# One scan instruction instead of two for the transposed states of a selective-scan kernel, their old states added in PSUM

## The chip, the cores and the metric

The kernel runs on one core of a Trainium2 chip. The metric is the device time of one execution in microseconds (us). The engines of the core are called PE (TensorE matmul), PEld (TensorE weight load), DVE (VectorE), ACT (ScalarE), POOL (GpSimd) and SP (SyncE, which issues most of the DMAs). Each runs its own instructions in order and waits for the others on semaphores.

## The reference, cut to what matters

The reference has two layers on an image of 256 x 256 tokens and 128 channels. Layer 0 is attention along the rows. Layer 1 is a two-dimensional selective scan: the tokens, widened to 256 channels, are walked in four orders (rows, columns, and both reversed), 65536 tokens in each. For each order, channel d and state n of 16:

```
delta = softplus(dts + dt_bias)
h[d, n] = exp(delta[d] * A[d, n]) * h[d, n] + delta[d] * x[d] * B[n]     # one token after the other
y[d]    = sum over n of h[d, n] * C[n] + D[d] * x[d]
```

The four outputs are added, normalised, gated and projected back to 128 channels. All of it is float32. The change lies in the recurrence of layer 1.

## The kernel before, in words

Layer 0 and the front of layer 1 (projection, convolution) come first; the scan stage starts some 5.5 ms into the execution and lasts to the end. It walks the four orders one after the other (`ORDER = (2, 1, 3, 0)`). An order has 128 chunks of T = 512 tokens; `steps[q]` is the order k and the first token a of chunk q. A chunk is done in NG = 8 groups (g) of 32 channels. The 128 partitions of a group are 4 quarters of the states times 32 channels, and each partition carries NI = 4 states i, so that 4 x 4 = 16 states are covered. One (q, g) is a step of the main loop (L1133); there are 4 x 128 x 8 = 4096.

The four states of a step lie in one tile `hs` (pool name `bx`) of 128 x 4 x 512. They are made in two ways:

- **States 0 and 1** (NB = 2). PE spreads delta*x over the partitions (`spread_du`, L878, into the PSUM tile `ur`), DVE multiplies it by the replicated B (`times_B`, L888). POOL adds the old state, multiplied by the decay of the first token, to column 0 (L1123). ACT writes the decays exp(delta*A) to the PSUM tile `dA`, 2 x 512 columns, of which column 0 of both states stays zero (L1107). DVE then scans both states in one instruction of 1024 columns (L1189): a zero decay in column 512 cuts the second state off from the first.
- **States 2 and 3**, the transposed ones. ACT forms their products with the tokens on the partitions (`products`, L851, into `bt`), and PE turns them back with four transposes for each state (`turn_back`, L863) into the PSUM tiles `bl0` and `bl1`, one bank and one buffer each. ACT writes their decays to `dAl` in SBUF (`long_decay`, L1107). DVE scans each state by its own instruction of 512 columns (L1172), with the old state `hst` as the initial value.

After its scans, POOL saves the last column of the four states, times `a0x`, in `hst` (L1193) and multiplies `hs` by the replicated C (L1196). `a0x` holds the first token's decay for states 0 and 1 and ones for states 2 and 3 (L797, L822). PE sums the products over the states into `yp` (`sums`, L902), two pieces of a chunk of four parts each.

The order of instructions is written out by hand (`manual_schedule`): a step has four places, n = 0 to 3, and `place = 4 * g + n` counts the 32 of a chunk. At n = 0 and n = 1 the half-scans are issued, each followed by the refill of its bank for the next step; at n = 2 `times_B` of the next step and `spread_du` of the one after; at n = 3 the scan of states 0 and 1. The work around the scan comes at fixed places, ahead of the scan of the place: `prepare` of the chunk after next (transposes `tps` at places 8 and 9, `pb` at 12, `pv` at 17 and 18, softplus at 19, which has its own table load, `tpb` and `tpd` from 27 on), the sums at 4 to 7 and 20 to 23, and `store` (`tpy` at 13 and 15) or, in the last order, `finish`, which also normalises, gates and projects. `SHARE` says how many instructions of `products` ACT issues at each place.

PSUM has 8 banks: `bl0`, `bl1`, `ur` and `yp` have one each, `dA` two, and the tag `mm` two buffers for all else. The weights `xw_in` and `dtw_s` of all four orders are loaded once, at the start of the stage.

Of the kernel before, what the change touches and what calls it, by code (L numbers as in the profile page):

```python
# [8 lines left out]
F32 = mybir.dt.float32  # L9
# [7 lines left out]
P = 128  # L17
# [6 lines left out]
DI = 256  # L24
NS = 16
R = 8
# [40 lines left out]
def attention_and_scan_kernel(  # L67
# [590 lines left out]
    NI = 4  # L658
    NB = 2
    sw = ctx.enter_context(tc.tile_pool(name="sw", bufs=1))  # L660
    xw_in = sw.tile([P, K, 2, R + 2 * NS], F32, name="xw_in")
    nc.scalar.dma_start(xw_in, x_projT)
    dtw_s = sw.tile([R, K, DI], F32, name="dtw_s")
    nc.scalar.dma_start(dtw_s, dt_wT)
    dtb_s = sw.tile([P, K, 2], F32, name="dtb_s")
    nc.scalar.dma_start(dtb_s, dt_b)
    A_s = sw.tile([P, K, 2, 4, NI], F32, name="A_s")
# [49 lines left out]
        v = ap.rearrange("(i p w) d -> p w i d", p=P, w=S)  # L717
        return [v[:, w, :, :] for w in range(w0, w0 + T // S)]

    loaded, prepared, summed, replicas, products_of = {}, {}, {}, {}, {}  # L720

    def load(q):
        k, a = steps[q]
# [7 lines left out]
    def prepare(q):  # L731

        k, a = steps[q]
        xt = loaded.pop(q)
        xs = io.tile([P, 2, T], F32, name="xs", bufs=3)
        tps = []
        for h in range(2):
            yield 8 + h
            tp = sps.tile([P, T], F32, name="tps", tag="mm")
            for j in range(4):  # L740
                nc.tensor.transpose(
                    tp[:, j * P : (j + 1) * P], xt[:, j, h * P : (h + 1) * P], ident
                )
            tps.append(tp)
        for h, tp in enumerate(tps):
            yield 10 + h
            nc.scalar.copy(xs[:, h, ::-1] if k >= 2 else xs[:, h, :], tp)  # L747
        yield 12
        pb = sps.tile([R + 2 * NS, T], F32, name="pb", tag="mm")
        for h in range(2):  # L750
            nc.tensor.matmul(  # L751
                pb, xw_in[:, k, h, :], xs[:, h, :], start=(h == 0), stop=(h == 1)
            )
        yield 14
        bc = io.tile([R + 2 * NS, T], F32, name="bc", bufs=1)
        nc.scalar.copy(bc, pb)
        bc_d = sd.tile([2 * NS, T], F32, name="bc_d")
        nc.sync.dma_start(bc_d, bc[R:, :])
        pvs = []
        for h in range(2):  # L760
            yield 17 + h
            pv = sps.tile([P, T], F32, name="pv", tag="mm")
            nc.tensor.matmul(  # L763
                pv, dtw_s[:, k, h * P : (h + 1) * P], bc[:R, :], start=True, stop=True
            )
# [12 lines left out]
        de0 = io.tile([P, NG, 1], F32, name="de0", bufs=1)  # L778
        if a:
            for j in range(4):  # L780
                nc.sync.dma_start(
                    de0[32 * j : 32 * j + 32],
                    de_d.rearrange("(g c) t -> c g t", c=32)[:, :, 0:1],
                )
        yield 27
        tp = sps.tile([P, 4, R + 2 * NS], F32, name="tpb", tag="mm")
        for b in range(4):
            nc.tensor.transpose(
                tp[:, b, :], bc[:, b * P : (b + 1) * P], ident[: R + 2 * NS, : R + 2 * NS]
            )  # L790
        B_t = io.tile([P, 4, R + 2 * NS], F32, name="B_t")
        tpbs = tp
        first = a0x[:, q % 2, :, :NB]
        tps = []
        for w in range(2):
            if w == 0 and a:
                nc.gpsimd.tensor_tensor(  # L797
                    first,
                    A_s[:, k, :, :, :NB].rearrange("p h q i -> p (h q) i"),
                    de0.to_broadcast([P, NG, NB]),  # L800
                    ALU.mult,
                )
# [12 lines left out]
        duT = io.tile([P, 4, DI], F32, name="duT")  # L815
        for w, tp in enumerate(tps):
            yield 30 + 2 * w
            nc.scalar.copy(duT[:, 2 * w : 2 * w + 2, :], tp)
        prepared[q] = xs, de_d, duT, bc_d, B_t
        yield 33  # L820
        if a:
            nc.scalar.activation(first, first, AF.Exp)  # L822
# [32 lines left out]
                    )  # L855
                    yield

    def turn_back(q, g, i):

        bl = sps.tile([P, T], F32, name=f"bl{i}", bufs=1)  # L860
        bt = products_of[q][i]
        for b in range(4):
            nc.tensor.transpose(  # L863
                bl[:, b * P : (b + 1) * P], bt[:, b, g].rearrange("t j c -> t (j c)"), ident
            )
        return bl

    def spread_delta(q, g):
# [228 lines left out]
    load(2)  # L1097
    begin_sums(0, 0)
    replicating, multiplying, summing = [], [], []
    bls = {(0, 0, i): turn_back(0, 0, i) for i in range(NI - NB)}  # L1100


    dA = sps.tile([P, NB, T], F32, name="dA", bufs=1)
    nc.vector.memset(dA[:, :, 0:1], 0.0)

    def decay(to, q, g, i, t0):
        nc.scalar.activation(  # L1107
            to,
            drs[q, g][:, t0:],
            AF.Exp,  # L1110
            scale=A_s[:, steps[q][0], g // 4, g % 4, i : i + 1],
        )

    def long_decay(q, g, i):
        dAl = wk.tile([P, T], F32, name="dAl")
        decay(dAl, q, g, i, 0)
        dAls[q, g, i] = dAl

    def begin(q, g):
        hs = wk.tile([P, NI, T], F32, name="bx", bufs=7)  # L1120
# [3 lines left out]
        bxs[q, g] = hs  # L1124

    SHARE = (0, 2, 2, 2, 2, 1, 2, 2, 2, 1, 1, 2, 1, 2, 1, 1, 0, 0, 0, 0, 0, 0, 2, 2, 1, 1, 1, 1, 0, 0, 0, 0)
    bxs, dAls = {}, {}
    for i in range(NB, NI):
        long_decay(0, 0, i)
    begin(0, 0)  # L1130
# [2 lines left out]
    for s, (q, g) in enumerate(all_steps):  # L1133
# [5 lines left out]
        for n in range(4):  # L1139
            place = 4 * g + n  # L1140
            if n < NB:
                decay(dA[:, n, 1:], q, g, n, 1)
            if nxt and n in (1, 2):
                long_decay(*nxt, NB + n - 1)
            if place == 0 and q + 2 < NQ:
                add_part(q, prepare(q + 2))
            if place == 1 and q + 1 < NQ:
                multiplying.append(products(q + 1))
            if place == 26 and q + 3 < NQ:
                load(q + 3)  # L1150
            if place == 10 and q + 1 < NQ:
                replicating.append(replicate(q + 1))
            if place == 28:
                evacuate(q, 0)
# [12 lines left out]
            piece(replicating)  # L1167
            for _ in range(SHARE[place]):
                piece(multiplying)
            if n < NI - NB:  # L1170
                i = NB + n
                nc.vector.tensor_tensor_scan(  # L1172
                    hs[:, i, :],
                    dAls.pop((q, g, i)),
                    bls.pop((q, g, n)),
                    0.0 if a == 0 else hst[:, g, i : i + 1],
                    ALU.mult,
                    ALU.add,
                )
                if nxt:  # L1180
                    bls[(*nxt, n)] = turn_back(*nxt, n)
            elif n == 2:
                if nxt:
                    begin(*nxt)
                if s + 2 < len(all_steps):
                    urs[all_steps[s + 2]] = spread_du(*all_steps[s + 2])
            else:
                run = hs[:, :NB, :].rearrange("p i t -> p (i t)")
                nc.vector.tensor_tensor_scan(  # L1189
                    run, dA.rearrange("p i t -> p (i t)"), run, 0.0, ALU.mult, ALU.add  # L1190
                )
# [72 lines left out]
```

## Time and profile before

| | |
|---|---|
| median of 3 runs | 29113.9 us (29111.15 to 29117.76) |
| the profiled execution | 29117.18 us, span 29115.4 us |
| mean granted PE clock | 0.934 |
| busy over the span | PE 87%, PEld 41%, DVE 92%, ACT 83%, POOL 80% |
| busy from 8000 to 20000 us (12000 us) | DVE 99.99%, ACT 92%, POOL 92%, PE 86% |
| DMA | 45.8% of 16 engines on SP's queue, 121 GB/s |

The parts of the scan stage, as the windows of the trace give them (busy us of each engine in the window; the fourth order starts near 23040 us):

```profile
core 0: us, PE busy (x) PEld busy (x) DVE busy (x) ACT busy (x) POOL busy (x), PEclk, DMA share, GB/s
...
11700.00:17500.00 5800.00, 5006.79 (x24601) 2168.01 (x24601) 5798.88 (x4103) 5326.92 (x10122) 5328.31 (x3319) 0.92 0.51 130
17500.00:23100.00 5600.00, 4847.66 (x23794) 2101.33 (x23792) 5599.04 (x3975) 5148.65 (x9784) 5146.00 (x3207) 0.92 0.51 130
23100.00:29115.00 6015.00, 5204.54 (x27327) 2561.11 (x27326) 5897.23 (x5016) 5650.60 (x10730) 5706.02 (x3879) 0.95 0.53 133
```

How to read it: after each engine's busy time stands the number of its instructions; `PEclk` is the clock that PE was granted, as a share of full speed. In the lines of the groups, `out<-in` are the program's tiles, then the shapes and the count, then the busy time and the mean of one in ns, then the idle time of the engine just before them and what ended it. In the lines in order of time the first number is the start in us from the span's start and the second the time to the end of the last of the merged instructions.

### The profile page before, as it was taken

The page shows a single profiled execution, that of the slowest core. Times are in us where ns is not written, and L with a number is a line of the kernel's source. Part 1 is how long each engine was busy: PE and PEld are TensorE (multiplying, and loading weights), DVE is VectorE, ACT ScalarE, POOL GpSimd, SP SyncE. Part 2 cuts the span into 40 slices and gives each one's busy share as a digit, 9 for nine tenths or more (in the row PEclk, how much of TensorE's full clock was granted, in tenths as well). Part 3 has the DMA queues.
Part 4 walks back from the last instruction along what each step waited for, and adds up shares of the span by engine and source line. Part 5 has one row for each costly group of instructions (what it writes and reads, how often), then busy time and mean ns, then how long its engine had stood idle before and what let it go on. Part 6 is the DMA issues. An engine that isn't in the chain of part 4 may idle for free. (4 is left out here: it accounts for less than half of the span.)

```text
span 29115.4 us, 414393 instructions
## 1 busy us (share of the span) xinstructions
PE 25211.6 (87%) x140314; PEld 11908.5 (41%) x140314; DVE 26672.0 (92%) x24930; ACT 24286.8 (83%) x47871; POOL 23266.7 (80%) x14327
## 2 busy tenths in 40 slices
PE   6999989888888888888888888888888888888888
PEld 2555545433333333333333333333333344444444
DVE  8666653599999999999999999999999999999999
ACT  5555542499999999999999999999999999999998
POOL 4222222499999999999999999999999999999999
PEclk8999999999999999999999999999999999999999
DMA  4001015555555555555555555555555555555554
GB/s 155 30 28 30 28 58 174 156 130 130 130 130 130 130 130 130 130 130 130 130 130 130 130 130 130 130 130 130 130 130 130 131 134 134 134 134 134 133 135 125
DMA packets 2737782, 3522.74 MB, mean 121 GB/s; under 512 B 707224, under 2 KB 1824280, under 8 KB 2659744
## 3 DMA queue, kind: packets, MB, share of 16 engines
q1 hardware_dynamic: 2730480, 3478.11, 45.8%
q8 instruction: 1102, 18.06, 0.3%
q10 hardware_dynamic: 5168, 18.12, 0.2%
q14 instruction: 1032, 8.45, 0.1%
HBM read 2689.15 MB, written 806.35 MB: 120 GB/s over the span
## 5 line engine op out<-in xcount | busy, mean ns | idle before, releaser
L1196 POOL TENSOR_TENSOR bx<-bx,C_r 128x2048 f32<-128x2048 f32 x4096 | 18644.2, 4552 | 336.3 <-DVE bx L1189 17.3
L1172 DVE TENSOR_TENSOR_SCAN bx<-dAl,hst,bl 128x512 f32<-128x512 f32 x8128 | 9875.5, 1258 | 0.0
L1189 DVE TENSOR_TENSOR_SCAN bx<-dA,bx 128x1024 f32<-128x1024 f32 x4096 | 9360.9, 2285 | 32.1 <-ACT dA L1107 31.6
L863 PE MATMUL bl<-ident,bt 128*128 128x128 f32 x32768 | 5605.3, 298 | 2280.1 <-DVE bx L1172 2247.7
L851 ACT ACTIVATE bt<-duT,B_t 128x256 f32<-128x256 f32 x16384 | 7394.4, 498 | 0.0
L1107 ACT ACTIVATE dA<-dr,A_s 128x511 f32<-128x511 f32 x8192 | 5598.4, 683 | 1505.8 <-DVE bx L1189 1433.8
L863 PEld LDWEIGHTS bl<-ident,bt 128*128 128x128 f32 x32768 | 3779.5, 149 | 6597.0 <-DVE bx L1172 6120.5
L1107 ACT ACTIVATE dAl<-dr,A_s 128x512 f32<-128x512 f32 x8192 | 5785.3, 712 | 170.3 <-DMA dr<-de_d 145.7
L878 PE MATMUL ur<-xs,spread 128*128 128x512 f32 x8192 | 5113.4, 710 | 410.6 <-DVE bx L888 401.0
L888 DVE TENSOR_TENSOR bx<-B_r,ur 128x1024 f32<-128x1024 f32 x4096 | 4915.1, 1200 | 66.1 <-DMA C_r<-bc_d 39.1
L902 PE MATMUL yp<-bx,gather 128*32 128x512 f32 x32768 | 4847.2, 649 | 68.3 <-POOL bx L1196 68.3
L370 POOL TENSOR_TENSOR at<-at,sm 128x2048 f32<-128x2048 f32 x256 | 922.3, 3603 | 2716.3 <-DVE sm L369 2607.1
L878 PEld LDWEIGHTS ur<-xs,spread 128*128 128x128 f32 x8192 | 1362.7, 209 | 2042.3 <-issue 957.6
L1193 POOL TENSOR_TENSOR hst<-bx,a0x 128x4 f32<-128x4 f32 x4064 | 820.3, 202 | 1272.6 <-DVE bx L1189 1269.3
L902 PEld LDWEIGHTS yp<-bx,gather 128*32 128x32 f32 x32768 | 694.1, 112 | 2445.1 <-issue 1800.0
L362 ACT ACTIVATE at<-at,mx 128x256 f32<-128x256 f32 x2048 | 1016.2, 498 | 474.1 <-DVE mx L358 469.4
L776 POOL TENSOR_TENSOR xs<-delta,xs 128x1024 f32<-128x1024 f32 x512 | 1217.0, 2377 | 45.6 <-ACT delta L770 45.6
L763 PE MATMUL pv<-bc,dtw_s 8*128 8x512 f32 x2048 | 1151.9, 642 | 45.5 <-ACT ys L976 43.4
L389 ACT COPY aT<-atp 128x512 f32<-128x512 f32 x512 | 299.7, 585 | 920.1 <-PE atp L382 581.4
L391 DVE COPY aT<-atp 128x512 f32<-128x512 f32 x512 | 353.7, 691 | 772.9 <-PE atp L382 762.4
L751 PE MATMUL pb<-xs,xw_in 128*40 128x512 f32 x2048 | 981.9, 602 | 19.3 <-ACT xs L747 19.1
L926 PEld LDWEIGHTS tpy<-ident,yo 128*128 128x128 f32 x6144 | 806.6, 192 | 367.3 <-issue 367.3
(168 smaller groups left out, 27475.4 us busy)
## 6 DMA issues: line engine op xcount, KB each, us to landing
dr<-de_d SPq DMA_DIRECT2D x4096, 256.0 KB
C_r<-bc_d SPq DMA_DIRECT2D x2048, 256.0 KB
de_d<-delta SPq DMA_DIRECT2D x512, 512.0 KB
B_r<-bc_d SPq DMA_DIRECT2D x2048, 128.0 KB
xtok<-xc_d SPq DMA_DIRECT2D x256, 512.0 KB
yl<-y_d SPq DMA_DIRECT2D x256, 512.0 KB
xtok<-xc_d SPq DMA_DIRECT2D x512, 256.0 KB
yl<-y_d SPq DMA_DIRECT2D x512, 256.0 KB
```

What stands on the lines that cost most here:

```text
L362: nc.scalar.activation(at[:, h, t, :], at[:, h, t, :], AF.Exp, bias=mx[:, h, t : t + 1], accum_out=sm[:, h, t : t + 1],)
L763: nc.tensor.matmul(pv, dtw_s[:, k, h * P : (h + 1) * P], bc[:R, :], start=True, stop=True)
L776: nc.gpsimd.tensor_tensor(xs, delta, xs, ALU.mult)
L851: nc.scalar.mul(bt[:, b, :, j, :], duT[:, b, :].rearrange("t (g c) -> t g c", c=32), B_t[:, b, n : n + 1],)
L863: nc.tensor.transpose(bl[:, b * P : (b + 1) * P], bt[:, b, g].rearrange("t j c -> t (j c)"), ident)
L878: nc.tensor.matmul(ur, spread[:, g % 4].rearrange("p j c -> p (j c)"), prepared[q][0][:, g // 4, :], start=True, stop=True,)
L888: nc.vector.tensor_tensor(bx[:, :NB, :], replicas[q][0], ur.unsqueeze(1).to_broadcast([P, NB, T]), ALU.mult,)
L902: nc.tensor.matmul(yp[32 * g : 32 * g + 32, :], gather, hc[:, i, :], start=(i == 0), stop=True, skip_group_check=True,)
L1107: nc.scalar.activation(to, drs[q, g][:, t0:], AF.Exp, scale=A_s[:, steps[q][0], g // 4, g % 4, i : i + 1],)
L1172: nc.vector.tensor_tensor_scan(hs[:, i, :], dAls.pop((q, g, i)), bls.pop((q, g, n)), 0.0 if a == 0 else hst[:, g, i : i + 1], ALU.mult, AL ...
L1189: nc.vector.tensor_tensor_scan(run, dA.rearrange("p i t -> p (i t)"), run, 0.0, ALU.mult, ALU.add)
L1196: nc.gpsimd.tensor_tensor(hs, hs, replicas[q][1], ALU.mult)
```

## The change

States 2 and 3 get one scan of 1024 columns as well (at n = 0). For this, column 0 of both decays must be zero and the old state must already be in the scan's input. `bl` becomes one tile of two banks with one buffer, refilled in one go at n = 1. After the four transposes of a state, `turn_back` writes column 0 again with an ordinary matmul of the same products (weights `bt`, moving operand the first column of the identity) and adds the old state with a second matmul (weights the identity, moving operand one column of `hst`). At the first chunk of an order both are left out. `a0x` now holds the decay of the first token for all four states, so that `hst` comes out multiplied for states 2 and 3 too. The decays go to two fixed tiles `dAl0` and `dAl1` (2 x 512 columns each, by the parity of g) from column 1 on. To make room in SBUF, `x_projT` and `dt_wT` are no longer held for all orders, but loaded for each order on SP's queue, at the start of `prepare` of its first chunk.

```diff
-    xw_in = sw.tile([P, K, 2, R + 2 * NS], F32, name="xw_in")
-    nc.scalar.dma_start(xw_in, x_projT)
-    dtw_s = sw.tile([R, K, DI], F32, name="dtw_s")
-    nc.scalar.dma_start(dtw_s, dt_wT)
...
         xt = loaded.pop(q)
+        if a == 0:
+            dtw[k] = io.tile([R, DI], F32, name="dtw", bufs=2)
+            nc.sync.dma_start(dtw[k], dt_wT[:, k, :])
+            xw_in[k] = io.tile([P, 2, R + 2 * NS], F32, name="xw_in", bufs=2)
+            nc.sync.dma_start(xw_in[k], x_projT[:, k])
...
-        first = a0x[:, q % 2, :, :NB]
+        first = a0x[:, q % 2]
...
-                    A_s[:, k, :, :, :NB].rearrange("p h q i -> p (h q) i"),
-                    de0.to_broadcast([P, NG, NB]),
+                    A_s[:, k].rearrange("p h q i -> p (h q) i"),
+                    de0.to_broadcast([P, NG, NI]),
...
-    def turn_back(q, g, i):
-
-        bl = sps.tile([P, T], F32, name=f"bl{i}", bufs=1)
-        bt = products_of[q][i]
-        for b in range(4):
-            nc.tensor.transpose(
-                bl[:, b * P : (b + 1) * P], bt[:, b, g].rearrange("t j c -> t (j c)"), ident
-            )
+    def turn_back(q, g):
+
+        bl = sps.tile([P, NI - NB, T], F32, name="bl", bufs=1)
+        for i, bt in enumerate(products_of[q]):
+            for b in range(4):
+                nc.tensor.transpose(
+                    bl[:, i, b * P : (b + 1) * P],
+                    bt[:, b, g].rearrange("t j c -> t (j c)"),
+                    ident,
+                )
+            if steps[q][1]:
+                nc.tensor.matmul(
+                    bl[:, i, 0:1],
+                    bt[:, 0, g].rearrange("t j c -> t (j c)"),
+                    ident[:, 0:1],
+                    start=True,
+                    stop=True,
+                    skip_group_check=True,
+                )
+                nc.tensor.matmul(
+                    bl[:, i, 0:1],
+                    ident,
+                    hst[:, g, NB + i : NB + i + 1],
+                    start=False,
+                    stop=True,
+                    skip_group_check=True,
+                )
         return bl
...
+    dAls = [sw.tile([P, NI - NB, T], F32, name=f"dAl{e}") for e in range(2)]
+    for dAl in dAls:
+        nc.vector.memset(dAl[:, :, 0:1], 0.0)
...
     def long_decay(q, g, i):
-        dAl = wk.tile([P, T], F32, name="dAl")
-        decay(dAl, q, g, i, 0)
-        dAls[q, g, i] = dAl
+        decay(dAls[g % 2][:, i - NB, 1:], q, g, i)
...
-            if n < NI - NB:
-                i = NB + n
+            if n == 0:
+                run = hs[:, NB:, :].rearrange("p i t -> p (i t)")
                 nc.vector.tensor_tensor_scan(
-                    hs[:, i, :],
-                    dAls.pop((q, g, i)),
-                    bls.pop((q, g, n)),
-                    0.0 if a == 0 else hst[:, g, i : i + 1],
+                    run,
+                    dAls[g % 2].rearrange("p i t -> p (i t)"),
+                    bls.pop((q, g)).rearrange("p i t -> p (i t)"),
+                    0.0,
                     ALU.mult,
                     ALU.add,
                 )
+            elif n == 1:
                 if nxt:
-                    bls[(*nxt, n)] = turn_back(*nxt, n)
+                    bls[nxt] = turn_back(*nxt)
```

The order of all other instructions stays: PE's refill of both halves now stands at n = 1, behind PE's work of the places n = 0 and n = 1.

More of the change, by code (lines that the diff above doesn't have):

```diff
@@ L718, in tokens @@
         return [v[:, w, :, :] for w in range(w0, w0 + T // S)]
-    loaded, prepared, summed, replicas, products_of = {}, {}, {}, {}, {}
+    loaded, prepared, summed, replicas, products_of, dtw, xw_in = ({} for _ in range(7))
     def load(q):
@@ L751, in prepare @@
             nc.tensor.matmul(
-                pb, xw_in[:, k, h, :], xs[:, h, :], start=(h == 0), stop=(h == 1)
+                pb, xw_in[k][:, h, :], xs[:, h, :], start=(h == 0), stop=(h == 1)
             )
@@ L763, in prepare @@
             nc.tensor.matmul(
-                pv, dtw_s[:, k, h * P : (h + 1) * P], bc[:R, :], start=True, stop=True
+                pv, dtw[k][:, h * P : (h + 1) * P], bc[:R, :], start=True, stop=True
             )
@@ L1099, in attention_and_scan_kernel, with decay @@
     replicating, multiplying, summing = [], [], []
-    bls = {(0, 0, i): turn_back(0, 0, i) for i in range(NI - NB)}
+    bls = {(0, 0): turn_back(0, 0)}
     dA = sps.tile([P, NB, T], F32, name="dA", bufs=1)
     nc.vector.memset(dA[:, :, 0:1], 0.0)
-    def decay(to, q, g, i, t0):
+    dAls = [sw.tile([P, NI - NB, T], F32, name=f"dAl{e}") for e in range(2)]
+    for dAl in dAls:
+        nc.vector.memset(dAl[:, :, 0:1], 0.0)
+    def decay(to, q, g, i):
         nc.scalar.activation(
             to,
-            drs[q, g][:, t0:],
+            drs[q, g][:, 1:],
             AF.Exp,
@@ L1126, in attention_and_scan_kernel @@
     SHARE = (0, 2, 2, 2, 2, 1, 2, 2, 2, 1, 1, 2, 1, 2, 1, 1, 0, 0, 0, 0, 0, 0, 2, 2, 1, 1, 1, 1, 0, 0, 0, 0)
-    bxs, dAls = {}, {}
+    bxs = {}
     for i in range(NB, NI):
@@ L1141, in attention_and_scan_kernel @@
             if n < NB:
-                decay(dA[:, n, 1:], q, g, n, 1)
+                decay(dA[:, n, 1:], q, g, n)
             if nxt and n in (1, 2):
```

## The prediction

> **What bounds the kernel now.** I read the page's busy shares first, then the groups of the scan stage (8000 to 20000 us, three of its four parts look alike), then the waits there, then ten-microsecond windows, and last the order of time on PE and DVE. Words: a step is one chunk (q) and one channel group (g = 0 to 7); 4 orders x 128 chunks x 8 groups make 4096 steps. "Refill" is the work of turn_back, eight transposes into bl.
>
> The groups (count, then busy and mean, then idle before):
>
> ```profile
> L1172 DVE TENSOR_TENSOR_SCAN bx<-dAl,hst,bl 128x512 f32<-128x512 f32 x4213 | 5124.6, 1261 | 0.0
> L1189 DVE TENSOR_TENSOR_SCAN bx<-dA,bx 128x1024 f32<-128x1024 f32 x2122 | 4856.7, 2289 | 0.8 <-issue 0.4 <-ACT dA L1107 0.4
> ...
> L788 PEld LDWEIGHTS tpb<-ident,bc 40*128 40x128 f32 x1060 | 85.3, 138 | 201.0 <-ACT bt L851 190.4 <-ACT dAl L1107 10.6
> ...
> L1172 DVE TENSOR_TENSOR_SCAN bx<-dAl,bl 128x512 f32<-128x512 f32 x32 | 36.9, 1198 | 0.0
> ```
>
> DVE has under 2 us of idle time in 12000: it sets the pace here. DVE in order of time gives that pace:
>
> ```profile
> 12040.57 2.42 DVE L1172 TENSOR_TENSOR_SCAN bx<-dAl,hst,bl 128x512 f32<-128x512 f32 x2
> 12042.91 1.19 DVE L888 TENSOR_TENSOR bx<-B_r,ur 128x1024 f32<-128x1024 f32 x1
> 12044.02 2.27 DVE L1189 TENSOR_TENSOR_SCAN bx<-dA,bx 128x1024 f32<-128x1024 f32 x1
> 12046.22 2.42 DVE L1172 TENSOR_TENSOR_SCAN bx<-dAl,hst,bl 128x512 f32<-128x512 f32 x2
> ```
>
> From start to start: the two 512-column scans 2.34 us, times_B 1.11, the 1024-column scan 2.20, a step 5.65. A record outlasts its pitch by some 0.09 us, so pitches are what I add up. Next, how much room PE has. Windows (PE, PEld, DVE, ACT, POOL busy, then PE's granted clock):
>
> ```profile
> 12040.00:12050.00 10.00, 9.58 (x45) 5.37 (x44) 10.00 (x9) 9.98 (x21) 8.51 (x6) 1.00 0.60 120
> 12050.00:12060.00 10.00, 10.00 (x49) 2.79 (x49) 10.00 (x8) 9.93 (x16) 9.16 (x8) 0.83 0.52 158
> ```
>
> PE has no room in these 20 us, and in the second ten its clock is 0.83: 1.7 us of its work lost. In order of time it runs from group 3 into group 7 with hardly a wait:
>
> ```profile
> 12041.87 0.66 PE L863 MATMUL bl<-ident,bt 128*128 128x128 f32 x4 [0.41 <-DVE bx L1172]
> 12042.36 1.02 PE L924 MATMUL tpy<-yl,ident 128*128 128x512 f32 x2
> 12043.23 1.05 PE L926 MATMUL tpy<-ident,yo 128*128 128x128 f32 x8
> 12044.12 0.60 PE L863 MATMUL bl<-ident,bt 128*128 128x128 f32 x4
> 12044.55 1.02 PE L878 MATMUL ur<-xs,spread 128*128 128x512 f32 x2
> ...
> 12049.75 1.12 PE L763 MATMUL pv<-bc,dtw_s 8*128 8x512 f32 x2
> 12050.80 1.39 PE L878 MATMUL ur<-xs,spread 128*128 128x512 f32 x2
> ...
> 12055.02 1.06 PE L902 MATMUL yp<-bx,gather 128*32 128x512 f32 x8
> 12056.02 0.66 PE L863 MATMUL bl<-ident,bt 128*128 128x128 f32 x4
> ...
> 12057.60 1.12 PE L878 MATMUL ur<-xs,spread 128*128 128x512 f32 x2
> 12058.66 1.06 PE L902 MATMUL yp<-bx,gather 128*32 128x512 f32 x8
> ```
>
> So DVE is the bound, but PE is a close second in one stretch of each chunk, and rests elsewhere. The change takes from DVE and gives to PE.
>
> **DVE, removed.** Two scans of pitch 1.17 become one of 1024 columns. The nearest row is L1189: the same width, one operand in PSUM, no state operand, pitch 2.20. A second bound: the 32 half-scans without hst are 63 ns shorter (1198 against 1261), 2 x (1.17 - 0.063) = 2.21. I take 2.20, so 0.14 us a step; 0.14 x 4096 = 573 us if DVE stays the bound. At worst the merged scan costs as much as the pair: 0. The step's floor becomes 5.51.
>
> **PE, added.** Each step gets four more matmuls of one column with 128x128 weights (a chunk at column 0 has none: 32 steps). A float32 matmul that is no transpose shows as two passes, each with its weight load (L878: 8192 of each for 4096 calls), so eight loads and eight one-column passes a step. A one-column pass streams next to nothing; the load sets its price. What a full load takes shows where one waits for the other:
>
> ```profile
> 12045.59 0.30 PEld L924 LDWEIGHTS tpy<-yl,ident 128*128 128x128 f32 x2 [0.84 <-ACT bc L756]
> ```
>
> Two loads, 0.30 us together at a mean of 0.19: the second starts 0.11 after the first. L926 agrees from above, eight passes in 1.05 with 0.275 for one: (1.05 - 0.275)/7 = 0.11. So 8 x 0.109 = 0.87 us a step. Bounds: the 40-row transposed loads of L788, four in 0.33 at 0.138, pitch 0.064, give 0.51; the mean record of the loads of L878, 0.209, with no overlap gives 1.67. I take 0.87, the row with the same 128x128 float32 form. The transposes themselves stay: four in 0.43 (12044.12 to 12044.55), eight 0.87. A refill becomes 1.74 us of PE.
>
> [...]
>
> **The wait, moved.** Today the first half of bl is free after the first half-scan and is refilled under the second. Now both halves come free when the merged scan ends, and the next merged scan needs both 3.31 us later (times_B 1.11, scan 2.20). Behind that wait in PE's queue stand spread_du, the yp sums, tpy and pv. The refill needs 1.74 plus 0.23 for the last pass to land (0.298 for a transpose against 0.109 pitch, and a signal), so it may start at most 1.35 us after its release, or DVE waits.
>
> Now PE's order with warm pitches from the rows: yp 1.00, ur 1.06, two tps 0.93, pb 1.85, tpy 1.76 or 1.93, pv 1.05, and 0.09 where a group with other tile sizes follows a refill. Zero is the end of group 1's merged scan; releases follow every 5.51.
> - Refill of 2: 0 to 1.74; border, yp, ur, yp 3.15; tps 0.93: 5.82. Release 5.51.
> - Refill of 3: to 7.56; ur 1.06, pb 1.85, tpy 1.76: 12.23. Release 11.02, late 1.21.
> - Refill of 4: to 13.97; ur 1.04, tpy 1.93, border and pv 1.14: 18.08. Release 16.53, late 1.55.
> - Refill of 5: to 19.82; border and pv 1.14, ur 1.06, two yp 2.00: 24.02. Release 22.04, late 1.98.
>
> Allowed is 1.35, so DVE loses 0.63 us a chunk at full clock, and with the 1.7 us that the clock takes in this very stretch 2.33. A chunk: 8 x 5.51 + 2.33 = 46.4 against 8 x 5.655 = 45.2: +1.2 us. Over the 384 chunks of the first three orders, +461 us.
>
> The clock fell to 0.83 in ten microseconds in which PE was busy 10.00. [...]
>
> The fourth order (L953, finish) has a step of 5.976 (502 scans of L1189 in 3000 us, 24500 to 27500), 47.8 a chunk, PE busy 0.87. PE's idle 6.2 us a chunk cannot hold 8 x 0.87 = 7.0, so at least +0.8; waits that the order forces remain, and I take the same +1.2: 128 x 1.2 = 154.
>
> **At nothing.** dA_l with 511 columns for 512, a0x 16 columns wider for each of POOL and ACT once a chunk (0.22 and 0.21 us rows; POOL and ACT are busy 92% there), no state read by DVE. Eight small loads on SP (dt_w and x_proj, two for each order) replace two on ACT's queue; they land long before pb. ACT's cover is thin: the second dA of group 5 ends near 12055.1, the scan starts 12055.33. If late pv holds softplus, up to 0.75 us a chunk, 380 us, comes on top; it stands in the upper end.
>
> **The sum.** The profiled execution took 29117 us (span 29115), 3 over the median 29114: 29117 + 461 + 154 = 29732, against the median 29730.
>
> **The rivals.**
> Faster: PE takes the passes in its gaps. It decides if a pass costs under about 0.064 or the clock stays at 1. With 0.51 a step the refill is 0.36 shorter, nothing is late at full clock and the slow clock costs 0.6: 44.08 + 0.6 is 0.56 below 45.24, x 512: 28830. Full clock with 0.87: 44.08 + 0.63, 0.53 below, 28845. All hidden: 29117 - 573, 28545. For it: weight loads of refills wait long for the scans in the 12000 us:
>
> ```profile
> PEld bl L863 <- DVE bx L1172: 3557.5, 2995, 3.1
> ```
>
> Against: that waiting lies in groups 0, 2 and 7, and PE cannot refill ahead of a scan, since bl has one buffer.
> Much slower: loads do not overlap at all, 1.67 a step. Allowed lateness 0.55, reached 1.98 + 3 x 0.8 = 4.4, stall 3.8 + 1.7, a chunk 49.6, 4.3 over: x 512, 31320.
> The merged scan is no cheaper than the pair: releases every 5.65, late 1.42, stall 0.1 + 1.7, chunk 47.0: 30040. L1189 speaks against it.
>
> **How the numbers follow.** Forecast, PE late in groups 3 to 6: 0.68, own range 29100 to 30600 (0.125 a pass instead of 0.109 adds 0.65 us a chunk, 333 us; ACT's 380). Faster rival 0.17, much slower or no cheaper scan 0.08; 0.07 for a balance within 0.2% (29056 to 29172), about what a measurement here tells from no change. The range reaches to the full clock at its low end and just past the forecast's own at its high end: 28840 to 30700.
>
> **What would show it.** Right: the merged scan at 2.2 us and DVE waits at it or at the dA scan for PE bl, mostly in groups 4 to 6, two us or more a chunk; the one-column passes 0.11 apart; that wait of PEld far below 3557. Wrong: DVE without gaps and a step of 5.51 (faster), passes 0.2 apart (much slower), a merged scan near 2.3, or DVE waiting for ACT with PE on time.

## The result and the profile after

The changed kernel took 29830 us (29807 to 29839, 4 runs) against 29114 (29111 to 29118, 4 runs): ratio 1.0244, 95% interval 1.0229 to 1.0259, that is 716 us slower. The forecast was 29730 in a range of 28840 to 30700. The profiled execution took 29807 us, 690 over that of before. Of the runs below, the one with the added passes on the kernel before has two executions in different states (32162 and 31333 us, mean clock 0.855 and 0.882), of which the faster is compared.

The costliest groups of the changed kernel that bear on the change, from its page (count, busy us, mean ns, idle time before and what ended it):

```profile
L1193 DVE TENSOR_TENSOR_SCAN bx<-dAl,bl 128x1024 f32<-128x1024 f32 x4096 | 9288.6, 2268 | 466.3 <-PE bl L878 419.0
L1211 DVE TENSOR_TENSOR_SCAN bx<-dA,bx 128x1024 f32<-128x1024 f32 x4096 | 9348.8, 2282 | 316.3 <-ACT dA L1130 291.1
...
L908 DVE TENSOR_TENSOR bx<-B_r,ur 128x1024 f32<-128x1024 f32 x4096 | 4916.3, 1200 | 539.3 <-PE yp L922 319.3
```

The merged scan (L1193) is as long as the scan of states 0 and 1, as forecast. But DVE, which had under 2 us of idle time from 8000 to 20000 us, now stands still before all three of its instructions. The waits of DVE from 8000 to 20000 us (total us, times, longest):

```profile
DVE bx L1193 <- PE bl L878: 218.0, 326, 1.6
DVE bx L1211 <- ACT dA L1130: 171.0, 200, 1.1
DVE bx L908 <- PE yp L922: 131.4, 196, 0.7
DVE bx L908 <- PE ur L898: 121.0, 187, 1.4
```

PE ends most of them: the refill (L878 is its last pass), the sums, the spread. The weight loads of the refill waited 3557.5 us for the scans before; now they wait half as long, so PE comes late to many of them:

```profile
PEld bl L864 <- DVE bx L1193: 1711.9, 955, 3.9
```

One crowded stretch, DVE in order of time:

```profile
12009.01 2.28 DVE L1211 TENSOR_TENSOR_SCAN bx<-dA,bx 128x1024 f32<-128x1024 f32 x1
12011.22 2.29 DVE L1193 TENSOR_TENSOR_SCAN bx<-dAl,bl 128x1024 f32<-128x1024 f32 x1
12014.90 1.22 DVE L908 TENSOR_TENSOR bx<-B_r,ur 128x1024 f32<-128x1024 f32 x1 [1.40 <-PE ur L898]
12016.41 2.29 DVE L1211 TENSOR_TENSOR_SCAN bx<-dA,bx 128x1024 f32<-128x1024 f32 x1 [0.29 <-ACT dA L1130]
12020.23 2.29 DVE L1193 TENSOR_TENSOR_SCAN bx<-dAl,bl 128x1024 f32<-128x1024 f32 x1 [1.53 <-ACT bt L852]
12023.19 1.22 DVE L908 TENSOR_TENSOR bx<-B_r,ur 128x1024 f32<-128x1024 f32 x1 [0.67 <-PE yp L922]
```

The 1.53 us before the scan at 12020.23 stand under ACT, but PE's last pass for it started after 12019.77. PE in the same stretch:

```profile
12008.23 1.12 PE L764 MATMUL pv<-bc,dtw 8*128 8x512 f32 x2
12009.28 0.65 PE L864 MATMUL bl<-ident,bt 128*128 128x128 f32 x4
12009.77 0.28 PE L870 MATMUL bl<-ident,bt 128*128 128x1 f32 x2
12009.92 0.36 PE L878 MATMUL bl<-hst,ident 128*128 128x1 f32 x2
12010.14 0.63 PE L864 MATMUL bl<-ident,bt 128*128 128x128 f32 x4
...
12011.04 1.81 PE L764 MATMUL pv<-bc,dtw 8*128 8x512 f32 x2
12012.79 2.08 PE L898 MATMUL ur<-xs,spread 128*128 128x512 f32 x2
12014.79 3.57 PE L922 MATMUL yp<-bx,gather 128*32 128x512 f32 x16
12018.30 0.65 PE L864 MATMUL bl<-ident,bt 128*128 128x128 f32 x4
...
12019.77 0.36 PE L878 MATMUL bl<-hst,ident 128*128 128x1 f32 x2
```

`pv` takes 1.81 us here and 1.12 three us earlier, `spread_du` 2.08 instead of 1.10 (at 12005.45), the sums 3.57 for 16 passes instead of 1.92 (at 12037.65): PE works at half its clock. Windows cut where the clock changes show it (PE busy is the first pair, the granted clock the number after POOL's):

```profile
12007.92:12011.34 3.42, 3.42 (x23) 2.52 (x22) 3.42 (x4) 3.02 (x5) 2.70 (x2) 1.00 0.54 189
12011.34:12014.75 3.41, 3.41 (x4) 0.50 (x2) 2.17 (x1) 2.04 (x3) 3.24 (x2) 0.50 0.16 57
12014.75:12018.16 3.41, 3.41 (x17) 0.60 (x16) 2.97 (x2) 3.37 (x7) 3.41 (x2) 0.50 0.51 168
12018.16:12021.57 3.41, 3.41 (x29) 2.20 (x26) 1.88 (x2) 3.41 (x8) 3.20 (x4) 1.00 0.53 117
```

PE has a record running in all of the first window, and the next two are granted 0.50. So the lost time in this stretch is not the length of the added passes, some 0.7 us in a step, alone.

The stretch is also the worst of four. From group 0's first scan to the next one, the chunks of the changed kernel last 45.01, 46.48, 50.80 and 45.45 us, over and over, and DVE stands still in them for 1.0, 2.1, 5.7 and 1.5 us; before, nearly every chunk took 45.24. The four together take 187.74 us, which is 55 windows of 3.413 us. The lines above are from the one of 50.80 (11981.51 to 12032.31). What costs the clock is the question that the experiments turned to.

### The profile page after: what moved, and what is told of

The parts are those of the page before. It is cut to its first block, busy times and chain, and to the rows that moved or that the text cites. A ratio compares the mean times of both kernels' runs of the same rounds, so it can differ in the third digit from the quotient of the medians.

```text
span 29805.5 us, 469790 instructions
## 1 busy us (share of the span) xinstructions
PE 27317.5 (92%) x172826; PEld 15781.5 (53%) x172826; DVE 26189.8 (88%) x20836; ACT 24337.1 (82%) x47871; POOL 23344.7 (78%) x14327
## 5 line engine op out<-in xcount | busy, mean ns | idle before, releaser
L1193 DVE TENSOR_TENSOR_SCAN bx<-dAl,bl 128x1024 f32<-128x1024 f32 x4096 | 9288.6, 2268 | 466.3 <-PE bl L878 419.0
L864 PE MATMUL bl<-ident,bt 128*128 128x128 f32 x32768 | 5449.3, 291 | 1530.8 <-DVE bx L1193 1529.6
L864 PEld LDWEIGHTS bl<-ident,bt 128*128 128x128 f32 x32768 | 4021.5, 157 | 3863.5 <-DVE bx L1193 2810.0
L1130 ACT ACTIVATE dAl<-dr,A_s 128x511 f32<-128x511 f32 x8192 | 5790.9, 713 | 80.0 <-DMA dr<-de_d 77.6
L922 PE MATMUL yp<-bx,gather 128*32 128x512 f32 x32768 | 4709.6, 659 | 120.3 <-POOL bx L1218 120.0
L878 PE MATMUL bl<-hst,ident 128*128 128x1 f32 x16256 | 3051.5, 257 | 0.0
L878 PEld LDWEIGHTS bl<-hst,ident 128*128 128x128 f32 x16256 | 2601.2, 201 | 0.0
L870 PEld LDWEIGHTS bl<-ident,bt 128*128 128x128 f32 x16256 | 2588.7, 201 | 0.0
L922 PEld LDWEIGHTS yp<-bx,gather 128*32 128x32 f32 x32768 | 846.8, 117 | 2907.6 <-issue 2533.9
L870 PE MATMUL bl<-ident,bt 128*128 128x1 f32 x16256 | 2360.5, 214 | 0.0
L764 PE MATMUL pv<-bc,dtw 8*128 8x512 f32 x2048 | 1210.1, 672 | 1.5 <-ACT bc L757 1.5
```

What stands on the lines that cost most here:

```text
L864: nc.tensor.transpose(bl[:, i, b * P : (b + 1) * P], bt[:, b, g].rearrange("t j c -> t (j c)"), ident,)
L870: nc.tensor.matmul(bl[:, i, 0:1], bt[:, 0, g].rearrange("t j c -> t (j c)"), ident[:, 0:1], start=True, stop=True, skip_group_check=True,)
L878: nc.tensor.matmul(bl[:, i, 0:1], ident, hst[:, g, NB + i : NB + i + 1], start=False, stop=True, skip_group_check=True,)
L922: nc.tensor.matmul(yp[32 * g : 32 * g + 32, :], gather, hc[:, i, :], start=(i == 0), stop=True, skip_group_check=True,)
L1130: nc.scalar.activation(to, drs[q, g][:, 1:], AF.Exp, scale=A_s[:, steps[q][0], g // 4, g % 4, i : i + 1],)
L1193: nc.vector.tensor_tensor_scan(run, dAls[g % 2].rearrange("p i t -> p (i t)"), bls.pop((q, g)).rearrange("p i t -> p (i t)"), 0.0, ALU.mul ...
```

## The experiments

Three theories were set against each other. **A**: the added passes take PE's time in groups 3 to 6, and their length alone makes it late. **B**: the moved wait, one buffer of `bl` free only when the long scan ends, costs by itself. **C**: the clock falls where PE does little work in its array, however busy it shows, and that makes PE late. Ratios are to the kernel before, run beside it on the same chip.

### The merged scan without the added passes

The four one-column matmuls of `turn_back` are left out, so the old states of states 2 and 3 are missing.

```diff
-            if steps[q][1]:
-                nc.tensor.matmul(bl[:, i, 0:1], ..., ident[:, 0:1], start=True, ...)
-                nc.tensor.matmul(bl[:, i, 0:1], ident, hst[...], start=False, ...)
```

> The changed kernel without its four one-column matmuls a step; the old states of states 2 and 3 are left out. The merged scan and the single refill at its end stay. Theory A (PE is too late in groups 3 to 6 because the added passes lengthen each refill): the refill is 0.87 us again, it may start 3.29 - 0.87 - 0.23 = 2.2 us after its release, and the lateness of 1.98 falls by up to 3 x 0.77, so nothing is late. A chunk is 8 x 5.49 = 43.9 us against 45.2 before: 384 x -1.3 = -500 us in the first three orders, 0 to -160 in the fourth: 28450 to 28650, DVE without waits for bl. Theory B (the wait itself is the cost: both banks come free only at the end of one long scan and bl has one buffer): DVE still waits for bl, 29500 to 29850. Theory C (the clock: PE does too little array work, whatever the order): as A but with a remainder of up to 1 us a chunk, 28500 to 29000.

Measured: 28755 us, ratio 0.9869 (0.9840 to 0.9897). DVE's only wait of the stage, 8000 to 20000 us:

```profile
DVE bx L1194 <- ACT dA L1113: 114.5, 270, 0.8
```

The time is 105 us above A's band, with ACT's wait as what remains. B falls: the wait is where the change put it and costs next to nothing. The added passes cost 1075 us in all, 2.8 times the 383 that the merged scan gains here. It would gain more: on its page the same wait for ACT's second `dA` holds 224 us of the whole span, where the kernel before has 32. 383 + 192 = 575, near the 573 of the prediction.

### The added passes without the merged scan

The kernel before, with the same four matmuls of one column (a column of zeros in the place of the old state).

```diff
+        if steps[q][1]:
+            nc.tensor.matmul(bl[:, 0:1], ..., ident[:, 0:1], start=True, ...)
+            nc.tensor.matmul(bl[:, 0:1], ident, zero, start=False, ...)
```

> The kernel before with the same four one-column matmuls a step (column 0 written again, and a column of zeros added), the two half-scans and their two refills as they were. The output is that of the reference. Theory A: the added 0.77 us a step makes PE late here too, by 3 x 0.77 = 2.3 us more at the end of group 6; a half-refill may be 3.4 us late, so the refills themselves still hold, but pv comes late for softplus, which has some 1 us of slack: 0.5 to 1.5 us a chunk, 29350 to 29900. Theory B: the passes are not the cost and the wait has not moved: 29100 to 29160. Theory C: as A.

Measured: 31333 us in one execution, mean clock 0.882. It is 2200 us slower than before, far over every expectation. PE's free time in the kernel before, 14%, is about as long as the added passes (some 0.7 us a step, 3000 us); that they cost three quarters of their length is more than A forecast.

### The same with 128 columns instead of one

The first added matmul writes the block again in all its 128 columns, not only in the first. PE gets more to do, in the same number of passes. Once on the changed kernel:

```diff
-                    bl[:, i, 0:1],
+                    bl[:, i, 0:P],
...
-                    ident[:, 0:1],
+                    ident,
```

> The changed kernel in which the first added matmul of each state rewrites the whole first block (128 columns) instead of its first column; the result is the same, PE streams 127 columns more in two passes for each state, 0.11 us a pass instead of 0.07, some 0.15 us of PE time a step more. Theory A: PE is later still, 4 x 0.15 = 0.6 us a chunk, 384 x 0.6 = 230 us slower: 29950 to 30150. Theory C: the added columns count as array work, the clock falls less, and more work makes PE faster: 29000 to 29650 with a granted clock of 0.95 or more from 8000 to 20000 us.

Measured: 29144 us (29141 to 29158, 8 runs), ratio 1.0005 (0.9994 to 1.0017), mean clock 0.965. Its window of the stage, and DVE's waits there:

```profile
8000.00:20000.00 12000.00, 10944.41 (x67646) 6499.30 (x67646) 11683.84 (x6354) 11012.36 (x20913) 11034.91 (x6849) 0.96 0.51 130
```

```profile
DVE bx L1211 <- ACT dA L1130: 273.7, 264, 1.5
DVE bx L1193 <- ACT bt L852: 17.6, 95, 0.5
DVE bx L908 <- PE yp L922: 12.1, 69, 0.2
DVE bx L1193 <- PE bl L878: 9.4, 46, 0.2
```

And once on the kernel before, whose half-scans stay:

```diff
-                bl[:, 0:1], ..., ident[:, 0:1],
+                bl[:, 0:P], ..., ident,
```

> The kernel before with the four added matmuls a step (31333 us, the run e2), of which the first of each state now rewrites 128 columns instead of one. Theory A: 0.15 us a step more, slower than the run with one column: 31400 to 32100. Theory C: the clock, 0.80 to 0.88 in that run, comes back to 0.92 or more, and the time falls to 29200 to 30400.

Measured: 29654 us, ratio 1.0176 (1.0147 to 1.0206), mean clock 0.954.

Longer passes in the same places make the first kernel 686 us faster and the second 1679. A alone is out: by PE's time both had to be slower. In the changed kernel the waits for the refill go from 218 to 9 us and those for sums and spread from 252 to 12. What is left is ACT's, 274 us where the kernel without added passes has 114.5. Part of that is A's after all: PE's late `pv` holds up ACT's softplus,

```profile
ACT delta L771 <- PE pv L764: 143.0, 263, 0.7
```

a wait that is not there in these 12000 us before, nor without the added passes, and that holds 172.2 us in the changed kernel. This version stays 390 us above the one without added passes.

### `tpy` moved out of the crowd

The matmuls of `store` go from places 13 and 15 to 24 and 25, where PE has idle time, in the changed kernel and in the kernel before.

```diff
-            yield 13 + 2 * h
+            yield 24 + h
...
-            yield 16 + h
+            yield 26 + h
```

> The changed kernel with the PE work of store (tpy) moved from places 13 and 15 to 24 and 25 and its copies to 26 and 27, in the first three orders: 3.6 us of PE work out of the crowded groups 3 and 4 into the light group 6. All passes stay. Theory A: lateness of 1.98 at the refill of group 5 minus 3.6 is below zero, DVE waits no more than 0.5 us a chunk in groups 3 to 6; 8 x 5.49 + 0.5 = 44.4, 384 x -0.8 from before: 28700 to 28950. Theory B: the order does not matter, 29700 to 29850. Theory C: with tpy gone, groups 3 to 5 hold only pv, which uses 8 rows of the array, and transposes; the clock falls there longer (granted clock under 0.90 from 8000 to 20000 us), and the gain is lost: 29700 to 30500.

> The kernel before (no added matmul) with tpy moved from places 13 and 15 to 24 and 25 and its copies to 26 and 27 in the first three orders. Theory A: PE's total is the same and was in time, 29100 to 29250. Theory C: with tpy gone from groups 3 and 4 the clock falls there for longer, as in the run e3: granted clock below 0.90 from 8000 to 20000 us, 29400 to 31000.

Measured: 31240 us, ratio 1.0722 (1.0691 to 1.0753), and 30117, ratio 1.0335 (1.0305 to 1.0365). The windows of the stage, the changed kernel first:

```profile
8000.00:20000.00 12000.00, 10833.08 (x60557) 5927.43 (x60556) 10577.04 (x5692) 9913.47 (x18730) 9909.42 (x6132) 0.88 0.46 116
```

```profile
8000.00:20000.00 12000.00, 10248.60 (x48219) 4312.83 (x48212) 11458.42 (x8037) 10476.37 (x19837) 10461.09 (x6495) 0.88 0.49 123
```

Both had 0.92. `tpy` is twice ten passes over the whole array, 1.9 us each time, and taking them out of the stretch that was called too full makes the kernels slower by 1410 and 987 us. Both times lie far over A's band; the second is in C's, the first above it.

The second one is C's case. Slow clock fills 64% of group 4 and 75% of group 5, where the kernel before has 5% and 16%, and DVE's new waits lie in groups 5 and 6. The first one is mixed, since `tpy` now stands ahead of the refill for group 7. PE at full clock, and the scan that waits for it:

```profile
12021.26 1.02 PE L944 MATMUL tpy<-yl,ident 128*128 128x512 f32 x2
12022.12 1.05 PE L946 MATMUL tpy<-ident,yo 128*128 128x128 f32 x8
12023.01 0.60 PE L864 MATMUL bl<-ident,bt 128*128 128x128 f32 x4
```

```profile
12024.90 2.29 DVE L1193 TENSOR_TENSOR_SCAN bx<-dAl,bl 128x1024 f32<-128x1024 f32 x1 [1.98 <-PE bl L878]
```

DVE waits 6.03 us a chunk there, 3.38 more than in the changed kernel, and 1.98 of it is this wait. Over 384 chunks that is some 760 of the 1410 us, and it is a matter of place and PE's time, as in A.

### `pv` over all rows

In the changed kernel `pv` uses all 128 rows of the array, those below the 8 filled with zeros. Its number of columns stays.

```diff
-                pv, dtw[k][:, h * P : (h + 1) * P], bc[:R, :], start=True, stop=True
+                pv, dtw[k][:, h * P : (h + 1) * P], bc_all, start=True, stop=True
```

> The changed kernel with pv fed over all 128 rows of the array instead of 8: the weights of dt and the tile bc are padded with rows of zeros, the result and the 512 columns streamed are the same. Theory C (the clock falls where little of the array works, and pv with 8 rows counts for almost nothing): the slow-clock time after pv, in group 5, shrinks; the granted clock from 8000 to 20000 us rises from 0.92 to 0.94 or more and 0.5 to 1.3 us of the 2.6 us that DVE waits in a chunk go: 29300 to 29650. Theory A (PE's time alone, the clock being what it is): only the 0.09 us borders around pv go, 0.2 to 0.4 us a chunk: 29680 to 29800.

Measured: 29605 us, ratio 1.0159 (1.0130 to 1.0189): 226 us less, in C's range. But the mean clock of the stage is 0.91, not above the 0.92 of the changed kernel. Counted from the clock's records and from the start of each softplus, the changed kernel has slow clock mainly at 2 to 7 us and again at 16 to 29; here there is none in the first 13 us and more later. So in these runs it is not the mean clock that goes with the time, but whether the slow windows meet the stretch in which DVE depends on PE. Group 5 shows it: slow clock fills 35% of it in the changed kernel, nothing here and with 128 columns, 4% with one added matmul (below). The price has moved, too: DVE's waits in groups 5 and 6 fall from 2.0 to 0.7 us a chunk, those in group 2 rise from 0.45 to 1.2.

### One added matmul instead of two

The transpose of the block with column 0 comes last of the four, and the old state is added straight onto its output; the rewriting matmul goes. Run twice.

```diff
-            for b in range(4):
+            for b in (1, 2, 3, 0):
...
-                nc.tensor.matmul(bl[:, i, 0:1], ..., ident[:, 0:1], start=True, ...)
                 nc.tensor.matmul(bl[:, i, 0:1], ident, hst[...], start=False, ...)
```

> The changed kernel with one added matmul for each state in place of two: the block with column 0 is transposed last, and the old state is added onto the transposed column at once (start=False), so four one-column passes a step fall away. Theory A: a refill is about 0.37 us shorter; the 2.6 us that DVE now waits in a chunk (672 us in the 255 chunks from 8000 to 20000) fall by 4 x 0.37 = 1.5 to about 1.1; 43.9 + 1.1 = 45.0 against 47.0 now and 45.2 before: 28950 to 29200. Theory B: 29750 to 29850. Theory C: the passes do no array work, the clock stays; the gain is that of A.

> The one-matmul version a second time, for its interval: 28760 to 28880 by both theories. Where the run before it stood alone it was 28818 us.

Measured: 28818 us, ratio 0.9890 (0.9862 to 0.9919), and 28815, ratio 0.9889 (0.9873 to 0.9906). It is faster than both kernels, 320 us under before, and faster than either expectation. Its waits:

```profile
DVE bx L1203 <- ACT dA L1122: 112.8, 270, 0.8
DVE bx L900 <- PE yp L914: 11.6, 27, 0.7
DVE bx L1185 <- PE bl L870: 1.3, 8, 0.2
```

That is 63 us above the kernel with no added pass at all.

With the full-row `pv` on top of it:

> The one-matmul version with pv over all 128 rows (the rows below the 8 hold zeros), so that the step's slowest stretch gives the array full rows. The one-matmul version took 28818 us, its clock was 0.96 and DVE waited 0.47 us a chunk from 8000 to 20000 us, nearly all of it for ACT. By C the clock rises a little further and some of these waits go: at most 0.47 x 384 = 180 us, so 28640 to 28800. By A (PE's time and order alone) nothing is gained: pv's passes are no shorter, the weight loads are longer; 28810 to 28950.

Measured: 28797 us (28792 to 28799) beside 28815 (28813 to 28818) on the same chip, ratio 0.9883 (0.9868 to 0.9898): the fastest version here. It is 18 us faster and just inside C's band, again with a lower mean clock (0.947 against 0.954). The wait for the sums drops from 11.5 to 4.0 us; ACT's 115 stay.

### Wide, but written only once

The block with column 0 comes by an ordinary matmul of 128 columns alone, without its transpose.

```diff
-            for b in range(4):
+            for b in range(1 if steps[q][1] else 0, 4):
...
-                    bl[:, i, 0:1], ..., ident[:, 0:1],
+                    bl[:, i, 0:P], ..., ident,
```

> The first block of each state comes by an ordinary 128-column matmul instead of a transpose and a one-column rewrite; the old state is added by one more matmul as in the change. PE gets for each state two passes of 128 columns in the place of one transpose (0.11 us more each, 0.22 a step) over the one-matmul version, and is still 0.2 a step below the change. By A it lies between these two by PE's time (28818 and 29830): 28900 to 29400. By C the passes of 128 columns hold the clock at 0.96 or more, DVE waits as little as in the one-matmul version, and it takes 28720 to 28900.

Measured: 29432 us, ratio 1.0101 (1.0086 to 1.0116). This missed C's band by 530 us and A's by 30. It has two transposes a step *less* than the version with the rewrite in 128 columns, and takes 288 us more, with the stage's clock at 0.93 instead of 0.96. Windows cut at the changes of the clock: the version with the rewrite, which recovers after one slow window,

```profile
11989.53:11992.94 3.41, 1.11 (x5) 0.31 (x4) 3.41 (x3) 2.51 (x6) 2.81 (x4) 1.00 0.15 55
11992.94:11996.35 3.41, 3.41 (x17) 3.14 (x15) 3.41 (x3) 3.41 (x9) 2.78 (x4) 0.50 0.63 152
11996.35:11999.77 3.42, 3.42 (x27) 1.33 (x26) 3.42 (x3) 3.42 (x8) 3.42 (x1) 1.00 0.45 92
```

and this one, which does not:

```profile
12032.26:12035.67 3.41, 0.96 (x3) 0.13 (x2) 3.41 (x3) 2.13 (x4) 3.33 (x4) 1.00 0.17 64
12035.67:12039.08 3.41, 3.34 (x15) 3.27 (x16) 3.41 (x4) 3.41 (x10) 3.05 (x2) 0.50 0.50 117
12039.08:12042.50 3.42, 3.42 (x14) 0.60 (x16) 3.42 (x3) 3.42 (x8) 3.25 (x2) 0.50 0.45 114
```

In both, PE is idle for most of the first window, and the second is slow. In it both do a refill and start `spread_du`, here with a shorter refill and 0.07 us of idle time (PE busy 3.34 against 3.41), and the clock stays down for a third window, in which the sums run slow. So "wide passes help" does not cover this pair. What goes with the slow windows may be the array work inside the window ahead; from this pair alone that is a guess, and the next part counts it.

### The count behind it

To see whether this holds beyond one pair, I took 8000 to 20000 us of eleven profiles (before, after, and all runs but the added passes without the merged scan and the repeat) and cut them into the 3.413 us windows in which the clock changes. Each matmul pass got a work, an estimate of mine, in units of one 128x128 block: (columns streamed / 128) x (share of the rows) x (share of the array's columns). That is 1 for a transposed block, 4 for a pass of `spread_du`, 1 for one of the sums, 0.25 for one of `pv`, 0.008 for a one-column pass. It was spread from the record's start over the time in which the columns stream, 0.107 us a block at full clock (a pass of 512 columns of `tpy` has a pitch of 0.429 us there, four times that, and one of `spread_du` 0.853 us where 0.50 is granted, eight times that), so that by this measure a window holds 32 at most, or 16 at 0.50. Then I counted how many windows are slow, by the work of the window ahead of each:

```
work in the window ahead   windows    slow
under 9                       3223    3210
9 to 13                       4683    2660
13 and more                  30742       0
```

With one bound at 12 the work of one window tells the next one's clock in 97.8% of the cases; "never slow" is right in 84.8%. With the transposes counted as nothing the best bound (4) tells 92%, and so does the best bound on the time in which PE is busy (1.78 us). A record of PE running does not tell the two apart: of the windows with a record of PE running for over 99% of the time some 1600 hold under 12, and nearly all of these are followed by a slow one; some 20100 hold 13 or more, and none is. In the profiles before and after alone there are 7027 windows: 471 under 9, all followed by a slow one, 683 of 1112 from 9 to 13, and none of the 5444 with 13 and more; the bound at 12 is right in 98.2%. It is a count over records and not an experiment, but it fits what the runs did. The slow window of the version with the rewrite (from 11992.94) holds 13.2 and the next is fast; that of the version written once (from 12035.67) holds 12.6 and the next is slow. The window of the changed kernel from 12007.92, with a record of PE running all the time, holds 10.6. Of some 3510 windows, 768 are under 13 in the changed kernel, 447 with 128 columns and 467 with one added matmul.

## Why the prediction was right, and where its steps were off

- **DVE, removed.** Right. Start to start the merged scan takes 2.18 where nothing delays it (12026.53 to 12028.71), forecast 2.20; the step's floor is 5.49 instead of 5.51.
- **PE, added.** Right in kind, a little high. The added passes start 0.111 us after one another, as the load row said, except the second of L870, which starts 0.031 after the first: 0.031 + 3 x 0.111 = 0.364 a state, 0.73 a step instead of 0.87. The refill at 12003.81 takes 1.64, forecast 1.74. The four loads start 0.110 to 0.112 apart (12004.135 to 12004.469).
- **The wait, moved.** The place was right: DVE waits mostly from softplus on, in groups 4 to 6 (2.06 us a chunk), and for PE; another 0.45 lies in group 2, which I did not have. The size was too small. Chunks last 46.98 us on average instead of 46.4: the floor 8 x 5.49 = 43.92, waits of 672 us over some 255 chunks = 2.63, and some 0.4, most of it because a record after a stop does not overlap the one ahead of it (the one at 12011.22, which follows at once, does so by 0.07 us). So it is 3.06 over the floor, where the forecast had 2.33; against 45.24 that is +1.74 a chunk, +668 over three orders, where the forecast had +461. Part of the waits is for ACT, 171 us or 0.67 a chunk, which I had put only into the upper end (0.75). 0.42 a chunk of that is there without any added pass; the rest fits the late `pv`, for which softplus waits.
- **The term that failed: the slow clock as a fixed 1.7 us.** The prediction took what the clock cost in one window of before and added it to a stall from full-speed pitches. That the two together came near the measured mean was partly luck. The clock's price is not a constant beside the added passes: the same number of passes cost 2200 us on the kernel before, 523 with 128 columns, and half as many on the merged scan cost 63 (28818 against 28755). Full-speed pitches alone give none of this. Nor is it a constant within the changed kernel, whose four chunks hold waits of 1.0, 2.1, 5.7 and 1.5 us. The other term, 0.63 us for a late refill at full clock, is not seen by itself either: with 128 columns a refill in the crowd at full clock takes 1.63 us (12010.97 to 12012.60), near the forecast's 1.74, and DVE waits 9.4 us for refills in the whole stage, 0.04 a chunk. There the length of the passes is felt through `pv` and softplus.
- **The fourth order.** Too high: +154 forecast, +28 measured, from 6139 to 6168 us between its first scan of states 0 and 1 and the end. Its step is 5.976 before, 5.991 after, 5.920 without the added passes. The changed kernel's window:

```profile
24500.00:27500.00 3000.00, 2821.76 (x17654) 1688.97 (x17654) 2877.37 (x2008) 2843.20 (x5385) 2858.02 (x1942) 0.98 0.54 134
```

  PE is busy for 2822 us in place of 2609, and its clock is 0.98 in place of 0.95. I had divided PE's idle time by the passes' length and did not ask what more work does to the clock. That the clock is why most of the cost is missing is argued, not tested.
- **The full clock, weighed against the row.** The estimate with the clock full in the crowd was 28845; against it stood the row of 12050 to 12060, with 0.83 granted and PE busy 10.00. From 8000 to 20000 us the slow stretches of both kernels last 3.41, 6.83 or 10.24 us and read 0.50. In the fourth order the clock did stay up, at 0.98. In the crowd it did not: the window from 12007.92 had PE busy throughout, and the next one was granted 0.50. Preferring the row there was right; turning the row into a constant was not.
- **The rivals.** "No cheaper" and "much slower" fell with the scan at 2.18 and the passes at 0.111. The faster rival was right about the room: with one added matmul instead of two the passes do disappear beside the scan, and 28818 is inside its 28545 to 28845.

## What to carry to other kernels

Before work is added to an engine that is a close second, see in the trace what its clock does there, and in which windows: in the changed kernel PE had a record running through all of the window from 12007.92, with one-column passes and a `pv` of 8 rows among them, and the next window was granted 0.50. Count added matmuls by passes for their time, 0.73 us a step for the eight here, and look at columns x rows beside the clock: with 128 columns in the place of one the changed kernel went from 29830 to 29144 us, so the longer pass was the cheaper one. And look for the version with fewer instructions first: adding onto the transpose's own output took away half of the added passes and with them nearly all of the loss (28818 us, against 28755 without any).

## What the runs showed of the hardware

- In the clock records of before and after all changes lie on a grid of 3.413 us, to within 0.001 us over the whole execution, wherever in a chunk they fall. Some periods here fit that grid: the version written once has slow stretches of 6.83, 3.41 and 3.41 us that repeat every 92.16 us, 27 windows, and its chunks last 46.12 and 46.04 in turn; four chunks of the changed kernel take 55 windows. The version with one added matmul does not quite fit it: its slow windows come every 13 (44.37 us) for up to 23 chunks of 44.43 on end and then slip. That a small change in a chunk's length moves where the slow windows fall is my reading of these periods and was not tested by itself.
- A slow window was followed by another one in the version written once (12035.67 to 12042.50, with 12.6 blocks in the first) and by a fast one in the version with the rewrite (from 11992.94, with 13.2).
- In the count, transposes go with the clock much like other passes of their size. In some 5900 windows the other passes alone come to under 9 and the transposes bring the sum to 13 or more; none of these is followed by a slow one (before and after alone: none of 1369), while 3210 of the 3223 with a sum under 9 are. No run here has transposes alone.
- In the version with one added matmul (28818 us) an ordinary float32 matmul adds onto the output of a PE transpose in PSUM, with the transpose of that block last of its bank. That was all the change needed: no second writing of column 0.
- Still open: what separates the windows with 9 to 13 blocks, and whether the counts look the same for other types and shapes; no run here varies the work of a window by itself.
